# A transformer layer on one core: first loads by half rows with V's products among the maxima, and last chunks in a new order with spread steps and buffers of their own

## The chip, the core and the metric

The kernel runs on one core of a Trainium2 chip. The core has a matrix engine (TensorE, PE in the profile, with PEld for its weight loads), a vector engine (VectorE, DVE), a scalar engine (ScalarE, ACT), GpSimd (POOL) and SyncE (SP), which here only issues DMAs. Each engine takes its instructions strictly in the order of the program; between engines semaphores say what must wait. DMAs are issued on SP's queue or on ACT's and are carried out by 16 DMA engines. The metric is the time of one execution in microseconds (us).

## The reference

One layer with 8 sequences of 1024 positions and width 256, everything in float32: attention with 16 heads of 16, with a fixed bell-shaped prior added to the scores, a residual and a layer norm without weights; then a feed-forward part with ternary weights, a low-rank branch and a squared ReLU, again with residual and norm. Cut to what matters:

```
Q, K, V = heads(x @ Wq.T + bq), heads(x @ Wk.T + bk), heads(x @ Wv.T + bv)
scores  = Q @ K.T / sqrt(16) + prior_lambda * gaussian_mask(L)
out     = softmax(scores) @ V                       # 16 heads
x       = layernorm(x + out @ Wo.T + bo)
h       = bitlinear(x, w_fc) + gate * (x @ v.T @ fast_b.T @ u.T)
r       = maximum(h, 0)
x       = layernorm(x + bitlinear(r * r, w_proj))
# bitlinear(x, w): s = mean|w| per row; x @ (clip(round(w / s), -1, 1) * s).T
```

## The kernel before

**Operands in parts.** Operands of many products are held as two float32r tiles: `hi`, the rounded value, and `lo`, what the rounding left. Queries and keys of four heads (a "group" G; 32 of them, four to a sequence) stand in the "stack": tiles `stack[name, s, pr, a]` (`st_q`, `st_k` in the profile) of 128 partitions by 1024 positions, two slots `s = G % 2`, each tile with one head's parts in 64 rows and two rows beside them for the row maxima. The parts go through DRAM: the projection gives a tile `two` (hi and lo), `write_parts` (L187 to L197) writes it to `parts_q` or `parts_k` in the order the stack needs (two DMAs for keys, three for queries), and `fill_stack` (L287) reads it back, 8 DMAs of 256 KB to a group.

**The start (L92 to L337).** x of sequence 0 is loaded in two halves (L99), the four weights on ACT's queue (L106), the biases behind the first x half on SP's queue. TensorE turns weights and x by transposes (`turn_weights`, `first_turn`), and `first_part` (L199) makes the key and query parts of the first eight heads, half by half of the positions: two ACT passes over the product (`full`, and `two`'s hi), then VectorE's subtraction for lo. The order of the calls is k and q of half 0, the second half of x, k and q of half 1. Only the parts of the first four heads are written at once; those of the next four (`second_heads`) are written after `fill_stack(0)`, whose key loads are on SP's queue and whose query loads are on ACT's. Then V for the whole of sequence 0 (L315 to L325: 32 matmuls, 8 additions of VectorE), `fill_stack(1)` and five small loads (L329 to L337). One of the `two` tiles of the start has the buffer named `junk`.

**The loop (L1463 on).** One pass `g` handles two blocks of 128 by 1024 exponentials (`exp_scores`, L698: matmuls L715, prior by matmuls L725 or by VectorE L738, exponential L739 on ACT) and the products with V of the pass before (`weigh`, L754). There are 512 passes. Twelve passes ahead (`LEAD`), `max_scores` (L634) makes the scores once more and `max_row` (L659) takes each row's maximum on VectorE, with an output tile nobody reads, also named `junk`; after every eight passes of this `set_max` (L671) transposes the maxima, negates them and sends them through DRAM into two rows of the query stack (one DMA out, L686, four back, L692). So the loop begins with 12 passes, g = -12 to -1, of maxima alone, the "lead-in".

**Pieces.** All other work (x transposes, projections, output projection, feed-forward) is cut into pieces `(cost, function, room, ready)` that stand in a list `jobs`. A pass takes pieces from the head while there is room (`halves`, the two halves of the PSUM bank `misc`) and the first one is ready. A piece issues its matmuls at once and returns `empty`, which issues the evacuation later in the pass. In the lead-in one piece is taken every second pass (two in the first): `load_x` of the next sequence and six of the eight key and query pieces of the second eight heads (`queries_keys`, L587). `defer(n, f)` puts a step off until n passes later. In the last 64 passes `own`, the list of pieces of the last sequence, follows when `jobs` is empty.

**The last sequence (`last_chunk`, L1109).** Its four chunks of 256 positions (e0 to e3) have pieces P (output projection, L1157, then VectorE's residual add L1160), T (transposes, L1185, to xhi and xlo), L (low-rank product, L1198, to `low`, L1211 on ACT and L1213 on VectorE), H (eight hidden pieces, L1236 with the low-rank term L1243; ReLU L1252 and square L1256 on ACT, product L1257 on GpSimd, lo L1258 on VectorE, once for two pieces) and O (two blocks of 128 positions in two parts each, L1272). After a block's second part VectorE multiplies and adds (L1281, L1282) and measures (L912, L913); after the second block GpSimd computes the inverse deviation of both (`norm_scale`, L917 and the power L918), and one unit later VectorE applies it to both (L1136) and one DMA writes 256 positions (L1290). Chunks 1 and 3 share buffers for xhi/xlo (`two`), `low` (the tile `prior`) and hi/lo (stack slot 0); chunks 0 and 2 share others.

**After the loop (L1545 on).** PSUM is one pool of eight banks, and the rest runs piece by piece in an order written out by hand: what is left of `own`, mixed with `divide_last(1)` (the last softmax sums, L874 to L899) and P of chunks 2 and 3; then H of chunk 1 with T and O of its neighbours, O of chunk 0, L of chunk 2 and so on, to H of chunk 3, O of chunk 2 and O of chunk 3. Every engine's instructions are tied to the order in which the program issues them.

## Time and profile before

| | us |
|---|---|
| median of three runs shown | 2251.11 (2249.8 to 2251.25) |
| profiled execution, its own time | 2246.88 |
| its span, first to last instruction | 2245.1 |
| first key and query loads of the stack issued | 23.75 |
| first matmul of the exponentials (L715, g = 0) | 69.58 |
| last products with V end | 2173.0 |
| last matmul ends | 2236.0 |

The granted TensorE clock is 0.99 on average over the span. How to read the lines shown: a line of the timeline has the start, the duration, the engine, the line of the kernel, the operation, the output and the inputs, the shapes, and the number of instructions that were merged (x4); in brackets stands how long the engine had been idle before it and what ended that. SPq and ACTq are the queues on which DMAs are issued, so that their lines show issues and not transfers. A line of a table of stretches has the stretch, its length, and for each engine its busy time in it and the number of instructions; then the granted clock (1.00 is full speed), the share of the DMA engines' time in use (just over 1 where packets overlap the edge of a stretch) and GB/s.

### The profile page before, as it was taken

Reading aid. Unit: us, or ns where it says so; the run is one execution under the profiler, and the core shown is the slowest. Engines: PE = TensorE matmul, PEld = TensorE weight load, DVE = VectorE, ACT = ScalarE, POOL = GpSimd, SP = SyncE. Lnnn points to the kernel's source line nnn. Section 1 sums busy time; section 2 is a strip of 40 time slices with the busy share of each in tenths; the row PEclk is TensorE's granted clock in tenths of the full one; section 3 lists DMA queues with packets and bytes.
Section 4 is the critical chain, followed back from the end, with each engine's and each line's share of the span. In section 5 each row is a group of like instructions: output and inputs, shape, how many; then the busy total and the mean of one; then the engine's idle time right before and its main releaser. Section 6 shows DMA issues by size and latency. Waiting matters only on the chain.

```text
span 2245.1 us, 36797 instructions
## 1 busy us (share of the span) xinstructions
PE 2167.9 (97%) x13144; PEld 1262.1 (56%) x13144; DVE 1591.8 (71%) x2959; ACT 1441.8 (64%) x2152; POOL 893.3 (40%) x1000
## 2 busy tenths in 40 slices
PE   6999999999999999999999999999999999999996
PEld 3444445565555655556555565555555555555556
DVE  5777777777777776777767777677777777677736
ACT  2466556766667667666666667676666666666654
POOL 3023232344324454344532444335443345345443
PEclk8899999999999999999999999999999999999998
DMA  8223233323343124423243223421344321422010
GB/s 204 91 76 109 59 73 124 90 72 71 100 116 105 37 74 116 131 68 78 69 131 104 73 67 89 131 85 52 74 119 122 78 73 52 139 56 58 23 35 20
DMA packets 110189, 193.36 MB, mean 86 GB/s; under 512 B 20973, under 2 KB 49981, under 8 KB 110005
## 3 DMA queue, kind: packets, MB, share of 16 engines
q1 hardware_dynamic: 108596, 188.91, 30.5%
q8 instruction: 104, 1.70, 0.3%
q10 hardware_dynamic: 1408, 2.10, 0.3%
q14 instruction: 81, 0.66, 0.1%
HBM read 105.19 MB, written 85.69 MB: 85 GB/s over the span
## 4 chain that ended last, share of the span: by engine, by line
PE 78%; DVE 8%; POOL 1%; ACT 1%; issue 1%; DMA 1%; SPq 0%; POOLq 0%; DVEq 0%; ACTq 0%
PE e L715 21%; PE av L754 18%; PE s L649 14%; DVE junk L661 5%; PE e L725 5%; PE misc L1028 4%; PE misc L1063 4%; PE misc L595 4%; PE misc L954 2%; PE misc L568 2%; PE misc L1035 1%; ACT exp L739 1%; DVE st L912 1%; PE misc L988 1%; PE misc L542 0%
## 5 line engine op out<-in xcount | busy, mean ns | idle before, releaser
L661 DVE CUSTOM_DVE_ANT_0 junk<-s,wide 128x1024 f32<-128x1024 f32 x1024 | 1248.7, 1219 | 534.7 <-PE s L649 483.7
L739 ACT ACTIVATE exp<-e 128x1024 f32<-128x1024 f32 x1024 | 1027.3, 1024 | 630.3 <-PE e L725 383.1
L715 PE MATMUL e<-st_q,st_k 66*128 66x512 f32 (+1 forms) x2048 | 666.1, 426 | 1.4 <-DVE pm L661 0.9
L715 PEld LDWEIGHTS e<-st_q,st_k 66*128 66x128 f32 (+1 forms) x2048 | 324.6, 189 | 464.4 <-ACT exp L739 81.8
L754 PE MATMUL av<-exp,v 128*17 128x512 f32 x4096 | 540.5, 599 | 0.0
L649 PE MATMUL s<-st_k,st_q 64*128 64x512 f32 x2048 | 403.6, 449 | 43.0 <-DVE pm L661 33.2
L649 PEld LDWEIGHTS s<-st_k,st_q 64*128 64x128 f32 x2048 | 168.1, 186 | 182.5 <-DVE pm L661 78.0
L738 DVE TENSOR_TENSOR e<-e,wide 128x372 f32<-128x372 f32 (+2 forms) x376 | 190.8, 508 | 53.9 <-PE e L715 48.6
L1046 POOL TENSOR_TENSOR rl<-rl 128x512 f32<-128x512 f32 x112 | 116.7, 1042 | 250.2 <-ACT hi L1045 243.7
L725 PEld LDWEIGHTS e<-prior,ident_r 128*128 128x128 f32 x1056 | 160.3, 190 | 24.3
L754 PEld LDWEIGHTS av<-exp,v 128*17 128x17 f32 x4096 | 68.0, 95 | 185.8 <-issue 183.1
L725 PE MATMUL e<-prior,ident_r 128*128 128x244 f32 (+2 forms) x1056 | 158.2, 272 | 0.0
L1048 POOL TENSOR_TENSOR lo<-rl,hi 128x512 fp32r<-128x512 f32 x112 | 145.4, 1298 | 8.8
L1083 POOL TENSOR_TENSOR r<-r,sp_row 128x256 f32<-128x256 f32 x56 | 41.1, 734 | 203.7 <-ACT r L1082 203.5
L578 POOL TENSOR_TENSOR v<-v,bv_row 128x256 f32<-128x256 f32 x56 | 38.5, 687 | 195.8 <-ACT v L577 195.8
L1028 PE MATMUL misc<-xhi,wfT 128*128 128x256 f32 x448 | 116.0, 282 | 0.2 <-ACT fullq L610 0.2
L1028 PE MATMUL misc<-xlo,wfT 128*128 128x256 f32 x448 | 115.1, 280 | 0.0
L1063 PE MATMUL misc<-wpT,lo 128*128 128x256 f32 x448 | 111.8, 283 | 2.1 <-POOL lo L1048 2.1
L1063 PE MATMUL misc<-wpT,hi 128*128 128x256 f32 x448 | 113.8, 287 | 0.0
L615 POOL TENSOR_TENSOR twok<-fullk,twok 128x512 fp32r<-128x512 f32 x30 | 39.0, 1300 | 187.1 <-ACT twok L614 187.1
L1041 ACT ACTIVATE rl<-misc,s_fc 128x256 f32<-128x256 f32 x224 | 94.1, 475 | 0.1
L1063 PEld LDWEIGHTS misc<-wpT,lo 128*128 128x128 f32 x448 | 85.0, 190 | 6.3 <-POOL lo L1048 2.9
(235 smaller groups left out, 2348.8 us busy)
## 6 DMA issues: line engine op xcount, KB each, us to landing
st_k<-parts_k SPq DMA_DIRECT2D x128, 256.0 KB
st_q<-parts_q SPq DMA_DIRECT2D x124, 256.0 KB
parts_k<-twok SPq DMA_DIRECT2D x60, 512.0 KB
parts_q<-twoq SPq DMA_DIRECT2D x64, 256.0 KB
parts_q<-twoq SPq DMA_DIRECT2D x30, 512.0 KB
x<-in_L_attn_x_dram SPq DMA_DIRECT2D x16, 512.0 KB
raw_o<-avs SPq DMA_DIRECT2D x248, 32.0 KB
rec<-back SPq DMA_DIRECT2D x30, 256.0 KB
```

Source lines behind the costliest of these rows:

```text
L649: nc.tensor.matmul(pair[a][:, kh, :], stack["q", s, pr, a][rows, ts(blk, P)], stack["k", s, pr, a][rows, ts(kh, HALF)], start=True, stop=True,
L661: nc.vector.tensor_tensor_reduce(out=junk, in0=t.rearrange("p k n -> p (k n)"), in1=wide[:, LEFT - P * blk : LEFT - P * blk + L], scale=1. ...
L715: nc.tensor.matmul(t[:, a, :], stack["k", s, pr, a][rows, ts(blk, P)], stack["q", s, pr, a][rows, ts(h, HALF)], start=True, stop=not by_pe,)
L725: nc.tensor.matmul(t[:, a, lo - HALF * h : hi - HALF * h], ident_r, prior[:, n, lo - first : hi - first], start=False, stop=(n == 1),)
L738: nc.vector.tensor_add(part, part, add.to_broadcast([P, 2, hi - lo]))
L739: nc.scalar.activation(e, t.rearrange("p a n -> p (a n)"), AF.Exp)
L754: nc.tensor.matmul(av[32 * j : 32 * j + HD + 1, :], v_bufs[b % 2][:, blk, g * HG + j, : HD + 1], es[j // 2][:, ts(j % 2, HALF)], start=(n ...
L1028: nc.tensor.matmul(ph, wfT[:, dc, ts(hc, P)], st[k2][:, dc, :], start=(dc == 0 and k2 == "xhi"), stop=False,)
L1041: nc.scalar.activation(rl[:, ts(k, n)], ph, AF.Relu, scale=s_fc[:, hc : hc + 1])
L1046: nc.gpsimd.tensor_mul(rl, rl, rl)
L1048: sub(lo, rl, hi.bitcast(F32))
L1063: nc.tensor.matmul(py, st[k][:, hc, ts(i, P)], wpT[:, hc, :], start=(hc == 0 and k == "hi"), stop=(hc == NHC - 1 and k == "lo"),)
```

## The change

**At the start.** Both halves of x are loaded first. Wq is scaled by 1/4 as it leaves PSUM, and the bias of q after it, so that no projection of q scales any more. `first_part` makes hi in one ACT pass and lo in one VectorE instruction from PSUM; the second half of x is turned between k and q of half 0, one of its four copies on VectorE. The four `two` tiles have the buffers `two`, one of the exponentials' (`e`), `o0` and `o1`. `fill_one` loads one stack tile or a range of its columns: for group 0 the keys whole on SP's queue and the first half of the queries on ACT's; then the last query part of half 1 is written, all parts of the next four heads, and the second half of the queries loaded.

**In the lead-in.** V of sequence 0 is made by the loop's own pieces (`values`: two matmuls in one bank half, an ACT copy, a GpSimd addition), taken in turn with the six key and query pieces and spread over the 12 passes; `load_x` of the next sequence stays in `jobs` for pass 0. The pieces stand behind the pass's scores and first maximum. `set_max` for the first eight passes comes one pass sooner, and half of its four loads go on ACT's queue. `fill_stack(1)` and the five small loads come at pass -2.

**At the end.** From seven passes before the last, `own` is mixed with what is left of `jobs`. Each block of 128 positions has its own inverse deviation, norm and output DMA; a block's residual add is measured at once; and an output's steps (multiply, add, measure, invert, finish) come 1, 2, 3, 5 and 6 units after its matmuls, for chunk 3 at once and one unit later. Chunk 3 gets `o0` and `rec` for xhi/xlo and `low`, chunk 2 stack slot 1 for hi/lo. The order after the loop is another: all T and L come ahead of the outputs, and the output parts of chunks 0 to 2 stand one by one between the hidden pieces of chunks 2 and 3.

```diff
     load_x(0, 0)
+    load_x(0, 1, "hi")
...
-    load_x(0, 1, "hi")
...
-    nc.vector.tensor_scalar_mul(bcol["q"], bcol["q"], qscale)
...
-        copy(t.rearrange("p c d -> p (c d)"), pt)
-        wT[name] = t
+        t = t.rearrange("p c d -> p (c d)")
+        if name == "q":
+            nc.vector.tensor_scalar_mul(t, pt, qscale)
+            nc.vector.tensor_scalar_mul(bcol["q"], bcol["q"], qscale)
+        else:
+            copy(t, pt)
...
-            nc.scalar.copy(xT[:, dc, ts(half, HALF)], pt)
+            copy = nc.vector.tensor_copy if dc == half == 1 else nc.scalar.copy
+            copy(xT[:, dc, ts(half, HALF)], pt)
...
-    def first_part(name, scale, half, tag, full):
+    def first_part(name, half, two):
...
+        nc.scalar.activation(two[:, 0, :], pt, AF.Identity, bias=bias)
+        nc.vector.scalar_tensor_tensor(
+            out=two[:, 1, :],
+            in0=pt,
+            scalar=bias,
+            in1=two[:, 0, :].bitcast(F32),
+            op0=ALU.add,
+            op1=ALU.subtract,
+        )
+        return two
...
-    turn_weights("q", nc.vector.tensor_copy)
-    first_part("k", 1.0, 0, "two", fulls[0])
-    first_part("q", qscale, 0, "junk", fulls[1])
+    turn_weights("q", None)
+    two = {}
+    def two_tile(name, half, pool, tag):
+        return pool.tile([P, 2, HALF], F32R, tag=tag, name=f"two{name}_0_0_{half}")
+    low, high = slice(0, P // 2), slice(P // 2, P)
+    two["k", 0] = first_part("k", 0, two_tile("k", 0, p1, "two"))
+    write_parts("k", parts_of["k", 0, 0], two["k", 0], 0, low)
     first_turn(1)
-    first_part("k", 1.0, 1, "o0", fulls[2])
-    first_part("q", qscale, 1, "o1", fulls[3])
+    two["q", 0] = first_part("q", 0, two_tile("q", 0, epool, "e"))
+    write_parts("q", parts_of["q", 0, 0], two["q", 0], 0, low)
+    two["k", 1] = first_part("k", 1, two_tile("k", 1, p1, "o0"))
+    write_parts("k", parts_of["k", 0, 0], two["k", 1], 1, low)
+    two["q", 1] = first_part("q", 1, two_tile("q", 1, p1, "o1"))
     turn_weights("v", nc.vector.tensor_copy)
     turn_weights("o", nc.scalar.copy)
     woT = wT["o"]
...
+    def fill_one(name, G, pr, a, queue, cols=slice(0, L)):
         (b, g), s = divmod(G, NG), G % SLOTS
-        assert made.get((b, g // 2)) == 2 * NHALF
+        at, src = P // 2 * a, HD * ((g % 2) * HG + 2 * pr + a)
+        queue.dma_start(
+            stack[name, s, pr, a][at : at + P // 2, cols].bitcast(F32),
+            parts_of[name, b, g // 2][src : src + HD, :, cols].rearrange("p l n -> (p l) n"),
+        )
...
+                for name in "kq":
+                    fill_one(name, G, pr, a, nc.sync)
+    halves_of_q = slice(0, HALF), slice(HALF, L)
+    for pr in range(NP):
+        for a in range(2):
+            fill_one("k", 0, pr, a, nc.sync)
+            fill_one("q", 0, pr, a, nc.scalar, halves_of_q[0])
+    write_parts("q", parts_of["q", 0, 0], two["q", 1], 1, low)
+    for (name, half), t in two.items():
+        write_parts(name, parts_of[name, 0, 0], t, half, high)
+    for pr in range(NP):
+        for a in range(2):
+            fill_one("q", 0, pr, a, nc.sync, halves_of_q[1])
+    def load_later():
+        nc.sync.dma_start(v_sb, v)
+        nc.sync.dma_start(fb_sb, fast_b)
+        nc.sync.dma_start(u_sb, u.rearrange("(c p) r -> p c r", p=P))
+        nc.sync.dma_start(gate_c, gate.partition_broadcast(P))
+        nc.sync.dma_start(bo_row, bo.partition_broadcast(P))
...
-                nc.sync.dma_start(row[at : at + 2, ts(h, HALF)], rows[:, j])
+                queue = nc.scalar if step == 0 and j % 2 else nc.sync
+                queue.dma_start(row[at : at + 2, ts(h, HALF)], rows[:, j])
...
+        def measure(mv, i, k):
+            norm_stats(st["r"], mv, i, f"{k}_{b}_{c}")
+        def invert(mv, i):
+            var = mv[:, i, 1:2]
+            nc.gpsimd.tensor_scalar_add(var, var, EPS)
+            nc.gpsimd.tensor_tensor(out=var, in0=var, in1=mhalf[:, :1], op=ALU.pow)
...
                 nc.vector.tensor_add(r[:, i, :], po, x1[:, i, :])
-                defer(1 + i, measure)
+                measure(mv, i, 1)
+                defer(1, lambda: invert(mv, i))
+                defer(2, apply)
+            def apply():
+                apply_norm(x1, mv, i)
                 if i == CT - 1:
-                    defer(2 + i, apply)
+                    st["normed"] = now
...
-                t = p1.tile([P, 2, NDC, n], F32R, tag="two", name=f"x12_{b}_{c}")
+                tag = "two" if c == 1 else "o0"
+                t = p1.tile([P, 2, NDC, n], F32R, tag=tag, name=f"x12_{b}_{c}")
...
-                if odd:
+                if c == 1:
                     t = prior.rearrange("p k n -> p (k n)")[:, :n]
                 else:
-                    t = p1.tile([P, n], F32R, tag="tern", name=f"low_{b}_{c}")
+                    tag = "rec" if odd else "tern"
+                    t = p1.tile([P, n], F32R, tag=tag, name=f"low_{b}_{c}")
...
-                    if odd:
-                        ab = [stack[name, 0, half, a] for a in range(2)]
+                    if c:
+                        ab = [stack[name, int(c == 2), half, a] for a in range(2)]
...
+                spaced = (1, 2, 3, 5, 6) if c < NCH - 1 else (0, 0, 0, 1, 1)
+                steps = multiply, add, lambda: measure(mv, i, 2), lambda: invert(mv, i), finish
+                for n, f in zip(spaced, steps):
+                    defer(n, f) if n else f()
+            def multiply():
                 nc.vector.tensor_mul(r[:, i, :], py, sp_row)
+            def add():
                 nc.vector.tensor_add(r[:, i, :], r[:, i, :], st["x1"][:, i, :])
+            def finish():
+                apply_norm(r, mv, i)
+                nc.sync.dma_start(out[b, ts(c * CT + i, P), :], r[:, i, :])
...
-                (0.23, lambda dc=dc: turn(dc), 1, lambda: st.get("normed", now) + 1 < now)
+                (0.23, lambda dc=dc: turn(dc), 1, lambda: "normed" in st)
...
+    v_first, qk_first, jobs[:7] = values(0, misc), jobs[1:7], jobs[:1]
+    early = [u for two in zip(v_first, qk_first) for u in two] + v_first[6:]
...
+        if g == -2:
+            fill_stack(1)
+            load_later()
...
-        if not jobs and g >= total - per_batch:
-            jobs, own = own, []
+        if g == total - 7:
+            old, jobs = jobs, []
+            while old and old[0][0] > 0.1 and old[0][2] == 0:
+                jobs.append(old.pop(0))
+            while old:
+                jobs += [own.pop(0), *old[:2]]
+                old = old[2:]
+            jobs, own = jobs + own, []
...
-        done = g + LEAD - 2
+        done = g + LEAD - (1 if g < 0 else 2)
...
         if g < 0:
-            if g % 2 == 0:
-                work += [jobs.pop(0)[1] for _ in range(2 if g == -LEAD else 1)]
+            n = g + LEAD + 1 - (done >= QSTEP - 1)
+            upto = 14 * n // (LEAD - 1)
+            if halves == 2:
+                work += [early.pop(0)[1] for _ in range(len(early) - 14 + upto)]
...
-        empties = [piece() for piece in work]
+        empties = [piece() for piece in work] if g >= 0 else []
         if g + LEAD < total:
             pair, blk, pm = max_scores(g + LEAD)
             max_row(pair[0], blk, pm[:, 0:1], f"{g + LEAD}_0")
+            if g < 0:
+                empties = [piece() for piece in work]
             rest = pair[1], blk, pm[:, 1:2], f"{g + LEAD}_1"
...
-    h1, h2, h3 = (k["H"] for k in (e1, e2, e3))
-    jobs = [*jobs[:1], last[0], *jobs[1:4], last[1], *jobs[4:6], *e2["P"], *jobs[6:8], *e3["P"], *jobs[8:]]
-    jobs += [*h1[:2], *e2["T"], *h1[2:4], *e0["O"], *e2["L"], *h1[4:], *e3["T"], *h2[:4]]
-    jobs += [*e1["O"], *e3["L"], *h2[4:], *h3, *e2["O"], *e3["O"]]
-    for u in jobs + [gap]:
+    h1, h2, h3, o0, o1, o2, o3 = (k[n] for n, k in zip("HHHOOOO", (e1, e2, e3, e0, e1, e2, e3)))
+    jobs = [*jobs[:1], last[0], *jobs[1:4], last[1], *jobs[4:7], *e2["P"], *jobs[7:8], *e3["P"], *jobs[8:]]
+    jobs += [*h1[:2], *e2["T"], *h1[2:4], *e2["L"], *e3["T"], *h1[4:6], *h2[:2], *e3["L"], *h1[6:]]
+    side = [*o0, *o1, *o2]
+    for k, u in enumerate(h2[2:] + h3):
+        jobs += [u, *(side[k : k + 1])]
+    jobs += [*side[k + 1 :], *o3]
+    for u in jobs + 7 * [gap]:
```

## The prediction

> **What bounds the kernel now.** I read the table of engines first, then stretches of the first 80 us and of the last 75 us, then single instructions in them. TensorE is busy 97% of the span, so the long middle is bound by matmuls and the change leaves it alone; only the two ends, where TensorE idles or runs at half clock, can give anything.
>
> ```profile
> PE 2167.9 (97%) x13144; PEld 1262.1 (56%) x13144; DVE 1591.8 (71%) x2959; ACT 1441.8 (64%) x2152; POOL 893.3 (40%) x1000
> ...
> 23.75 2.51 SPq L296 DMA_DIRECT2D st_k<-parts_k  x4
> 26.41 2.85 ACTq L296 DMA_DIRECT2D st_q<-parts_q  x4
> 32.55 0.47 PE L649 MATMUL s<-st_k,st_q 64*128 64x512 f32 x1 [1.90 <-DMA st_q<-parts_q]
> 38.34 1.23 DVE L661 CUSTOM_DVE_ANT_0 junk<-s,wide 128x1024 f32<-128x1024 f32 x1 [8.20 <-DMA parts_q<-twoq]
> ```
>
> See two waits in series. The first scores wait until 32.55 for the loaded queries. Then the first maximum waits until 38.34, although its scores lie ready: its output tile `junk` shares its buffer with the query part that was being written to DRAM, and that write stood in the queue behind the loads.
>
> ```profile
> core 0: us, PE busy (x) PEld busy (x) DVE busy (x) ACT busy (x) POOL busy (x), PEclk, DMA share, GB/s
> 28.00:38.30 10.30, 2.90 (x12) 1.35 (x10) 1.24 (x3) 0.47 (x1) 0.00 (x0) 0.80 0.96 266
> 38.30:69.50 31.20, 22.93 (x64) 11.01 (x64) 27.12 (x44) 4.64 (x10) 4.28 (x4) 0.72 0.74 195
> 69.50:75.20 5.70, 5.62 (x16) 3.85 (x16) 3.02 (x5) 2.52 (x3) 0.00 (x0) 0.50 0.35 133
> ...
> 2173.00:2180.00 7.00, 4.64 (x27) 4.01 (x28) 3.38 (x11) 2.17 (x5) 0.93 (x2) 0.84 0.00 0
> 2180.00:2204.50 24.50, 23.07 (x155) 19.68 (x153) 16.07 (x35) 12.56 (x28) 8.09 (x10) 0.98 0.01 1
> 2204.50:2208.50 4.00, 0.20 (x2) 0.00 (x0) 2.77 (x5) 1.18 (x4) 2.98 (x4) 1.00 0.00 0
> 2208.50:2219.30 10.80, 10.77 (x76) 10.57 (x76) 6.19 (x15) 5.50 (x12) 3.09 (x5) 0.84 0.08 26
> 2219.30:2222.00 2.70, 0.00 (x1) 0.00 (x0) 2.64 (x4) 0.89 (x2) 1.98 (x2) 1.00 0.00 0
> 2222.00:2236.00 14.00, 13.66 (x100) 13.46 (x100) 6.85 (x14) 5.92 (x12) 5.04 (x6) 0.88 0.06 20
> 2236.00:2245.10 9.10, 0.00 (x0) 0.00 (x0) 4.18 (x12) 0.00 (x0) 1.23 (x3) 0.68 0.16 58
> ```
>
> The columns are stretch, its length, busy time of each engine (instructions), granted clock, DMA. From 38.3 to 69.5 VectorE sets the pace: 24 maxima, 1.37 us from one to the next, 27.1 of 31.2 us busy. The first group of exponentials runs at clock 0.50. At the end there are two holes in TensorE (3.8 and 2.7 us), each followed by matmuls at a lowered clock, and 9.1 us after the last matmul. What makes a hole:
>
> ```profile
> 2205.79 1.04 POOL L1257 TENSOR_TENSOR rl<-rl 128x512 f32<-128x512 f32 x1
> 2205.86 2.16 DVE L1136 TENSOR_SCALAR xT<-xT,mv,rstd 128x256 f32<-128x256 f32 x2 [1.14 <-POOL rstd L918]
> 2208.53 0.58 PE L1243 MATMUL ph<-low,lowT 128*128 128x256 f32 x1 [3.84 <-DVE low L1213]
> ```
>
> VectorE waits in order 1.14 us for GpSimd's power, then needs 2.16 us for two normalizations beside GpSimd's products (the same two took 0.73 us at 2236.34 with GpSimd idle), and `low`, which TensorE needs, stands behind.
>
> **The lead-in, step by step.** The key part of half 0 takes one ACT pass instead of two: 11.54 + 0.69 (ACT) + 0.69 (DVE) gives its writes at 13.0 instead of 13.56. The second half of x is transposed before the queries (1.04 us of PE), so the query part is there at about 15.9 instead of 15.24; its three issues take 2.85 us (0.57 + 1.05 + 1.23), to 18.9, and the key part of half 1, ready at 17.9, is issued to 20.1. SP no longer issues the last query part (20.80 to 23.64) before the loads. A write landed 2.8 us after its issue (23.64 to ACT's 26.41), so the key loads start at 22.9 instead of 23.75, and the query halves on ACT's queue at 21.7 instead of 26.41. The first scores need two key tiles and two query halves. Before, 2 MB landed between 23.75 and 33.5, 215 GB/s. Until the second key tile there are 0.5 MB of keys and 0.5 MB of query halves, a quarter MB of them ahead of 22.9: 3.7 us, and some 1.7 us to land, gives 28.3; the maximum begins at about 29.0. The query part now lies in a buffer of the exponentials, so nothing holds `junk`: the 8.2 us wait goes. First maximum 38.34 to 29.0: **-9.3**. Bounds: 27 (no landing time) and 33 (the 6.1 us from issue to 32.55 taken from 22.9, and 4 us of DMA disorder): -11 to -5.
>
> Then twelve steps of two maxima. V's eight pieces now lie here: each 4 matmuls (1.02 to 1.13 us at full clock, 2.08 at half, the rows of L595, same shape), an ACT copy (0.47, row L610) and a GpSimd add (0.687, row L578) in place of VectorE's 0.42. VectorE's eight adds stood in the empty stretch 23 to 29, so dropping them saves nothing by itself. A step needs about 1.0 us of scores and 14/11 x 1.1 us of pieces, 2.4 us of PE at full clock against VectorE's 2.75: hidden, with PE 87% full; at half clock 4.4 to 4.8. As the pieces now stand behind the scores in PE's order, the small waits of the maxima (31.2 - 22 x 1.373 = 1.0 us) can go. Against that PE is empty from about 20 to 27.5, V having left that gap, and starts at half clock: in the trace, after PE stood from 34.2 to 38.3, the clock is 0.50 from 36 to 44 and full again from 46. Two steps at half clock cost 2 x (3.7 - 2.75) = 1.9. Net **+0.5**, bounds -1 to +6.
>
> [...]
>
> The row maxima's way back to the stack (set_max, PE 61.25, rows issued 63.38, second hop from 65.87, first exponential matmul 69.58: 8.3 us) now starts a step sooner by its number but still only when the eighth pair is done; two of its four hops go to ACT's queue, where V's copies wait behind them. `fill_stack(1)` (8 loads, 5 us of issue) and the five small loads move from before the lead-in to two steps before its end; behind them in SP's queue stand the next key part and the next batch's x. Group 4 needs the stack at about 78, it lands near 69; x lands near 75 and is wanted near 75, as `load_x` now comes first in group 0 and shifts the pieces by one group. Taken **+0.5**, bounds 0 to +4. With PE warm, the group at half clock (5.7 us from 69.5) takes about 4.5: **-1.2**, bounds -2 to 0. Lead-in: -9.3 + 0.5 + 0.5 - 1.2 = **-9.5**.
>
> **The end.** The work on PE after the last weighing (2173.0) at full-clock rows: 32 hidden pieces x 0.583, 16 output parts x 0.96, 4 projections x 1.69, transposes 1.8, low-rank 1.9, the last division 1.3: 46 us. It took 63.0, to 2236.0: 10.7 idle (stretches above), the rest, 6.3, lowered clock. The new order makes every low-rank product before the outputs, in tiles of their own, and an output's steps are spread over six units, so VectorE no longer waits for the power with `low` behind it. The two holes (6.5) go, and of the 2.4 idle us before 2180 I take 1.5, because chunk 0's transposes and low-rank now fit into groups 510 and 511: -8.0. Of 6.3 of lowered clock 2 stay: -4.3. Added: the last output part now waits for its own squares, with no other output between: ACT 0.47 + 0.63, GpSimd 1.04, VectorE 0.69 and hand-overs 0.3, less the 0.96 part in front: +2.2. VectorE becomes full: 36.5 us of its rows, plus up to 0.7 for each normalization beside GpSimd, in some 50 us, and GpSimd gets 8 more powers (0.94 each): +2.5, bounds 0 to +8. The drain: add, statistics and norm of one block instead of two, 128 KB last instead of 256: 9.1 to 6.7, -2.4. Loop lengthened by 0.6, products moved into it 0.9: -0.3. Tail: -8.0 - 4.3 + 2.2 + 2.5 - 2.4 - 0.3 = **-10.3**, bounds -16 to -3.
>
> **Sum.** -19.8: span 2245.1 to about 2225, the profiled execution 2246.88 to 2227. The median shown, 2251.11, lies 4.2 above that execution; I shift it alike: 2231.
>
> **Rivals.** (1) The loads stay the limit: DMA is 96% busy from 28 to 38, and the first scores come at 33 whatever the order. Against it: only half as many bytes are needed first, and the `junk` wait of 5.3 us behind the scores goes anyway. Lead-in -5, all 2236. (2) The end is bound by VectorE and the order of GpSimd's powers and products: single normalizations wait as the pairs did. For it: 16 waits where there were 8; against it: the spread leaves a power three units or more. Tail -3, all 2238. (3) Slower: the lead-in is bound by PE at half clock. Place: the twelve steps; price: a step takes 2.4/clock, 4.8 at 0.50, 11.5 x 2.05 = +23.6 against the term of +0.5, so 2254. It decides once the clock of the stretch is below 0.53. For it: 0.50 for most of the 10 us from 51; against it: the mean there is 0.72 with PE at 73%, and fuller stretches (75 to 80) run at 1.00. (4) The pieces don't come earlier, since `ready` refuses them in the last seven groups: about -2 less, inside the forecast's range.
>
> **How the numbers follow.** Forecast 0.66 (2223 to 2237), rival 1 0.10, rival 2 0.14, rival 3 0.06, and 0.04 for more gain than I see. The range for 8 in 10, with the bounds of start (-5) and end (-3) not both taken: 2220 to 2241. What a measurement tells from no change is 0.2%, 4.5 us: faster 0.91, within 0.03, slower 0.06.
>
> **What would show it.** First maximum near 29 with no DMA before it (step 1); maxima 1.37 us apart, clock over 0.8 from the third step (step 2); first exponential matmul near 60 (step 3); no hole over 1 us on PE between the last weighing and the last hidden piece, then one of about 2 us (end); about 6.7 us from the last matmul to the end. I am wrong if PE waits for x or the stack in groups 0 to 4, or if VectorE is over 90% busy in the end.

## The result, and the profile after

The changed kernel takes 2232.31 us (median of 4 runs, 2227.59 to 2233.07), the kernel before 2250.79 (4 runs, 2249.8 to 2251.25): a ratio of 0.991, 95% interval 0.9896 to 0.9924. The profiled execution took 2231.73, its span 2229.9, which is 15.2 us under the profile before; the prediction's sum was 19.8.

The engine line of the page after:

```profile
PE 2160.5 (97%) x13144; PEld 1258.9 (56%) x13144; DVE 1591.5 (71%) x2952; ACT 1442.7 (65%) x2155; POOL 902.7 (40%) x1024
```

And single instructions of its first 30 us (start, length, engine, line, tiles, the wait in front):

```profile
18.89 2.78 ACTq L298 DMA_DIRECT2D st_q<-parts_q  x4
21.60 2.42 SPq L298 DMA_DIRECT2D st_k<-parts_k  x4
...
25.78 0.76 PE L647 MATMUL s<-st_k,st_q 64*128 64x512 f32 x1 [8.73 <-DMA st_k<-parts_k]
...
27.74 1.22 DVE L659 CUSTOM_DVE_ANT_0 junk<-s,wide 128x1024 f32<-128x1024 f32 x1 [6.30 <-PE s L647]
```

Scores and maximum no longer wait in series for two transfers: the scores begin 6.8 us sooner (32.55 to 25.78), and the first maximum follows them at once, 10.6 us sooner (38.34 to 27.74).

The same stretches as before, of the profile after (length, busy time of each engine, granted clock, DMA share and GB/s):

```profile
20.00:27.70 7.70, 1.56 (x4) 0.78 (x4) 1.29 (x4) 0.00 (x0) 0.00 (x0) 0.60 0.95 235
27.70:59.60 31.90, 28.27 (x102) 16.16 (x101) 27.90 (x45) 7.17 (x17) 8.32 (x10) 0.88 0.70 197
59.60:65.30 5.70, 5.19 (x22) 3.04 (x21) 4.71 (x9) 4.14 (x6) 1.33 (x2) 1.00 1.08 201
2164.30:2171.60 7.30, 5.32 (x44) 5.02 (x42) 2.65 (x7) 4.14 (x10) 1.97 (x2) 1.00 0.00 0
2171.60:2184.00 12.40, 12.08 (x69) 8.98 (x67) 8.20 (x21) 5.20 (x12) 6.25 (x12) 1.00 0.01 1
2184.00:2186.20 2.20, 0.13 (x1) 0.00 (x0) 2.20 (x4) 0.84 (x2) 0.71 (x1) 0.86 0.00 0
2186.20:2192.40 6.20, 6.15 (x29) 6.15 (x30) 2.20 (x5) 3.73 (x8) 1.95 (x2) 0.50 0.00 0
2192.40:2214.90 22.50, 22.50 (x189) 22.28 (x188) 15.50 (x30) 13.29 (x27) 12.45 (x17) 1.00 0.06 20
2214.90:2219.90 5.00, 0.74 (x4) 0.53 (x4) 4.50 (x10) 0.27 (x1) 2.54 (x4) 0.98 0.09 33
2219.90:2223.60 3.70, 3.69 (x19) 3.69 (x19) 2.02 (x7) 0.00 (x0) 1.56 (x4) 0.56 0.08 27
2223.60:2229.90 6.30, 0.26 (x3) 0.05 (x1) 2.42 (x7) 0.00 (x0) 0.77 (x2) 0.73 0.18 62
```

The lead-in's maxima still take VectorE 27.9 us; TensorE beside them is fuller (28.3 of 31.9 us) at clock 0.88, and the first group of exponentials runs at 1.00 instead of 0.50. In the end the old holes of 3.84 and 2.70 us are gone, and there are new ones: 2.1 us at 2184, then half clock for 6.2 us, and 4.3 us in the five from 2214.9. While VectorE has 4.50 of 5.00 us of work there, TensorE stands.

Where the 15.2 us lie follows from the start of each group's first exponential, after against before: 10.7 us sooner at group 0, 12.7 at group 2, 13.2 at group 68, 9.3 at group 76, 10.0 at group 504, 9.0 at group 511. The span ends 15.2 sooner. So the lead-in gave 12.7, the place at groups 68 to 76 took 3.9 back, 1.2 were won elsewhere on the way, and from group 504 on 5.2. This is the place that took back:

```profile
348.19 0.47 PE L647 MATMUL s<-st_k,st_q 64*128 64x512 f32 x1 [0.94 <-PE misc L540]
348.60 0.62 ACT L612 CAST twoq<-fullq 128x512 fp32r<-128x512 f32 x1 [2.66 <-DMA parts_k<-twok]
349.12 1.93 ACT L738 ACTIVATE exp<-e 128x1024 f32<-128x1024 f32 x2
...
350.19 1.22 PE L647 MATMUL s<-st_k,st_q 64*128 64x512 f32 x3 [1.53 <-ACT exp L738]
```

ScalarE's rounding of the query parts (L612) waits until the key parts, which lie in the same buffer `two`, are written to DRAM. The exponentials stand behind it on ScalarE, the next scores wait for a bank that an exponential must free, and TensorE is empty for 1.53 us; then its clock is 0.51 for 6 us. The 0.94 us in front aren't due to this wait: they are as long where the rounding doesn't wait (`own_part` below, at 351.48). Before, the same wait is there, 1.44 us long (L614 at 360.62), TensorE is empty for 0.94 + 0.31 us, and the clock stays 1.00.

### The profile page after: what moved, and what is told of

It reads as the page before. It is cut to its first block, busy times and chain, and to the rows that moved or that the text cites. A ratio compares the mean times of both kernels' runs of the same rounds, so it can differ in the third digit from the quotient of the medians.

```text
span 2229.9 us, 36851 instructions
## 1 busy us (share of the span) xinstructions
PE 2160.5 (97%) x13144; PEld 1258.9 (56%) x13144; DVE 1591.5 (71%) x2952; ACT 1442.7 (65%) x2155; POOL 902.7 (40%) x1024
## 4 chain that ended last, share of the span: by engine, by line
PE 82%; DVE 8%; POOL 1%; issue 1%; ACT 1%; DMA 1%; SPq 0%; POOLq 0%; DVEq 0%; ACTq 0%
PE e L714 22%; PE av L753 19%; PE s L647 15%; DVE junk L659 6%; PE e L724 5%; PE misc L1027 4%; PE misc L593 4%; PE misc L1062 4%; PE misc L953 2%; PE misc L566 2%; PE misc L1034 1%; ACT exp L738 1%; DVE st L911 1%; PE misc L987 1%; PE misc L540 0%
## 5 line engine op out<-in xcount | busy, mean ns | idle before, releaser
L576 POOL TENSOR_TENSOR v<-v,bv_row 128x256 f32<-128x256 f32 x64 | 43.8, 686 | 213.4 <-ACT v L575 213.4
```

## The experiments

All times are set against runs of the kernel before on the same chip. "Tail" is the time from the start of the last weighing's matmuls (the last that read `exp` and `v`) to the span's end: 72.7 us before, 66.2 after.

**The changed kernel again, and each part alone.** No edit in the first; the second and third take the lead-in's or the end's lines of the diff.

> The changed kernel once more. In its first profile TensorE stood 2.47 us at 347 to 350 us (ScalarE's rounding L612 waits 2.66 us for the write of the key parts, exponentials behind it) and then ran at clock 0.50 to about 356: the lead over the kernel before falls there from 13.2 to 9.4 us. Theory C (chance: the DMA round trip in front of it fell late): in some executions the stall is as short as before, the times are of two kinds some 4 us apart, 2227.5 and 2232, and the profile may show either. Theory D (the change itself makes the stall): it is in every execution, all times 2231 to 2233.

Measured: 2229.72 (2226.86 to 2231.87), ratio 0.9912 (0.9891 to 0.9933). The four times are 2226.86, 2228.06, 2231.38 and 2231.87. The profile (2228.06) shows both places of interest once more, the first by instructions and the stretch behind them, the second by stretches:

```profile
347.47 0.62 ACT L612 CAST twoq<-fullq 128x512 fp32r<-128x512 f32 x1 [1.50 <-DMA parts_k<-twok]
...
349.07 0.73 PE L647 MATMUL s<-st_k,st_q 64*128 64x512 f32 x3 [0.37 <-DMA rec<-back]
...
350.00:353.40 3.40, 3.40 (x13) 1.70 (x6) 2.07 (x4) 1.58 (x3) 0.68 (x1) 0.50 0.87 309
```

```profile
2182.40:2184.60 2.20, 0.08 (x1) 0.00 (x0) 2.20 (x4) 0.86 (x3) 0.67 (x1) 1.00 0.00 0
2184.60:2190.80 6.20, 6.03 (x48) 5.79 (x49) 2.85 (x6) 5.64 (x14) 3.09 (x3) 1.00 0.00 0
```

The wait at L612 is 1.50 here, TensorE is empty for 0.94 + 0.37 us, the clock is halved for 3.4 us behind it where it was for 6.8, and 1.7 us are lost in place of 3.9. The hole in the end is as long as it was (2.13 us), and the clock behind it is 1.00 where it was 0.50: the tail is 64.2 instead of 66.2. Theory C fits: two profiles of the same program pay different prices at both places, and the four times fall into two pairs, though four times are few.

> The kernel before with the lead-in's part of the change alone (its end as before). By the traces the lead-in is worth 12.7 to 13.2 us up to group 68. Theory C: the median falls by that, 2238. Theory D: it gives 3.5 back in groups 68 to 76, 2241. By the prediction's own sum (-9.5): 2241 as well, but with the first maximum near 29 and the lead at group 20 at 9.5 and not 12.7. First exponential matmul near 59.7 in any case.

Measured: 2238.31 (2237.04 to 2239.29), 0.9951 (0.9932 to 0.997), 11 us under the kernel before. Its first maximum came at 29.98, and the lead was 9.1 us at group 2 and 11.1 at group 60, with nothing lost at groups 68 to 76 (11.4 behind them). The start varies: the first key part comes off TensorE at 10.19 us in the first profile of the changed kernel, at 10.71 in the second and at 11.86 here, and the first maximum follows it (27.74, 27.90, 29.98); what makes it vary is not shown.

> The kernel before with the end's part of the change alone. By the traces the end is worth 5.2 us (lead 10.0 at group 504, 15.2 at the end), of 10.3 predicted. If the two parts add up: 2245.5. Rival (the prediction's sum holds for the end and something of the lead-in's part took it away): 2240.5. In its profile the stretch after the last weighing has the steps of VectorE 3.5 us apart as in the changed kernel.

Measured: 2243.69 (10 runs, 2239.7 to 2246.33), 0.9971 (0.9961 to 0.9981), 5.7 us under the kernel before. Tail 63.9, the same holes as with the whole change (2.13, 2.19 and 2.08 us), and 1.1 us lost between group 504 and the last weighing. The profiled execution was the fastest of the ten. The parts add up: 11 + 5.7 is 16.7, the whole was 18.5 in the first comparison and 19.6 in the second, each to some 3 to 5 us by its interval.

**The lead-in: one buffer, the half rows, V.**

> The kernel before with one buffer moved: the query part of half 0 lies in a buffer of the exponentials instead of the maxima's. Nothing else. Theory: the first maximum waits only for its scores (33.04 instead of 38.34, matmuls 33.04 + 0.97), so it begins near 33.7 and all that follows comes 4.6 us sooner: 2246. Rival (the loads behind it or VectorE's next wait take the place): first maximum sooner, first exponential matmul still near 69.6, time within 1 us of 2250.8.

```
-    first_part("q", qscale, 0, "junk", fulls[1])
+    first_part("q", qscale, 0, "e", fulls[1], epool)
```

Measured: 2248.28 (10 runs), 0.9993 (0.9982 to 1.0004): no difference, as the rival has it. The first maximum came at 34.98, 3.4 us sooner, and the first exponential matmul at 68.06, 1.5 sooner. What took the place, in order of time on ScalarE and TensorE of this kernel:

```profile
59.98 0.62 ACT L614 CAST twoq<-fullq 128x512 fp32r<-128x512 f32 x1 [8.77 <-DMA parts_k<-twok]
60.50 0.47 ACT L610 ACTIVATE fullk<-misc,bk 128x256 f32<-128x256 f32 x1
...
61.02 0.38 PE L677 MATMUL misc<-ident,pm 128*16 128x128 f32 x1 [3.48 <-ACT fullk L610]
```

The rounding that waits at group 70 waits here too, 8.77 us, for writes issued at 53.7 and 54.8 that land at about 60, with DMA 0.88 to 0.95 busy up to 61. A key piece behind it holds the `misc` bank, and the transpose of the maxima waits for that bank. So the buffer alone gives nothing that shows: the transpose's results leave ScalarE at 61.44, where they left it at 61.67 before. The wait shown at L661 was the first of two that end at the same place.

> The changed kernel with the queries' rows loaded whole for the first group, behind the write of the second half, as before the change (all else of the lead-in as changed). The prediction's step: the half rows let the loads start at 18.9 instead of behind the write of half 1 (issued to 20.5, landed near 23.3), and a score came 6.1 us behind its loads' issue: first scores 29.5 instead of 25.8, first maximum 30.5 to 31 instead of 27.8, time +2.5 to +3 on 2229.7, 2232.5. Rival (the stretch is bound by DMA, 95% busy, and what comes first doesn't matter for the end of the lead-in): first exponential matmul within 1 us of the changed kernel's 59.7.

```
+    write_parts("q", parts_of["q", 0, 0], two["q", 1], 1, low)
     for pr in range(NP):
         for a in range(2):
             fill_one("k", 0, pr, a, nc.sync)
-            fill_one("q", 0, pr, a, nc.scalar, halves_of_q[0])
-    write_parts("q", parts_of["q", 0, 0], two["q", 1], 1, low)
+            fill_one("q", 0, pr, a, nc.scalar)
...
-            fill_one("q", 0, pr, a, nc.sync, halves_of_q[1])
```

Measured: 2235.14 (2231.7 to 2240.93), 0.993 (0.9908 to 0.9953). Query loads and first scores of this kernel:

```profile
25.05 2.85 ACTq L298 DMA_DIRECT2D st_q<-parts_q  x4
...
30.86 0.76 PE L643 MATMUL s<-st_k,st_q 64*128 64x512 f32 x1 [13.04 <-DMA st_q<-parts_q]
...
33.24 1.22 DVE L655 CUSTOM_DVE_ANT_0 junk<-s,wide 128x1024 f32<-128x1024 f32 x1 [11.33 <-PE s L643]
```

The first maximum is 5.3 us later than in the second profile of the changed kernel, and the first exponential matmul 4.0 (65.10 against 61.09). In the nine profiles with half rows and V beside the maxima these two lie from 27.74 to 29.98 and from 59.66 to 63.25, so the order of the bytes is worth 3.3 to 5.5 us of the one and 1.9 to 5.4 of the other. By the ratios it is some 4 us of the time, and their intervals overlap. It is more than expected at least in part because the three issues of the second query write take 3.8 us of SyncE (18.57 to 22.38) where those of the first took 2.1 (15.05 to 17.11), and the loads stand behind them.

> The changed kernel with V of the first sequence back in the gap in front of the lead-in (eight pieces on TensorE, VectorE adding the bias), the six query and key pieces left beside the maxima. The prediction's step: V beside the maxima is hidden and costs 0.5 at most for a cold clock, so V in the gap changes the time by -1 to +0.5: clock 1.00 at 20 to 28, no wait of 0.94 in front of the third maximum. Rival G (V in the gap delays the first scores, which stand behind it on TensorE, and the maxima, behind eight adds on VectorE): first maximum 1 to 3 us later, time by as much.

```
+    for tp in range(NB // 2):
...
-    early = [u for two in zip(v_first, qk_first) for u in two] + v_first[6:]
+    early = qk_first
```

Measured: 2231.03 (2229.1 to 2233.3), 0.9913 (0.9895 to 0.9931). First maximum 28.37, no wait before the third (maxima 1.38 apart), clock 1.00 at 20 to 28; 24 maxima take 32.56 us from first to last, against 32.46 and 32.65 in the two profiles of the changed kernel, and 32.66 before. Neither a cost nor a gain of V beside the maxima shows.

**The middle: the shared buffer.**

> The changed kernel with a buffer of their own for the query parts of the first two sequences (instead of the one that the key parts are written from), so that ScalarE's rounding L612 doesn't wait for the key parts' write, with the exponentials behind it. Between groups 60 and 100 the kernels with the changed lead-in lost up to 4.5 us against the profile before (3.8, 1.7, 4.6, 3.9, 2.4, 2.1 us, and 0.4 with the lead-in alone), always at that wait. Theory C (that wait alone, its length by chance): the loss between groups 60 and 100 is under 0.5 us and the time is some 2.5 us under the changed kernel's 2229.7 to 2232.3, 2228. Rival H (the wait only moves on to the next user of the buffers or of SyncE's queue): loss and time as they were.

```
-                two = p1.tile([P, 2, HALF], F32R, tag="two", ...)
+                two = p1.tile([P, 2, HALF], F32R, tag="lo" if name == "q" and b < 2 else "two", ...)
```

Measured: 2230.47 (2229.11 to 2236.61), 0.9928 (0.991 to 0.9946). In the profile L612 runs at 349.26 with no wait in front, and from group 68 to 76 the lead grows by 0.7 us. The profiled execution is the slowest of the four nevertheless: holes of 1.2 to 2.1 us elsewhere were followed by a low clock in it, such as this one at group 26, 1.96 us long in every profile with the changed lead-in; the first line is this kernel's, the second the changed kernel's in its second profile:

```profile
166.90:172.90 6.00, 6.00 (x29) 2.96 (x33) 3.12 (x6) 3.48 (x6) 0.00 (x0) 0.72 0.27 106
```

```profile
166.60:172.60 6.00, 5.96 (x38) 2.98 (x39) 4.64 (x10) 3.47 (x6) 0.00 (x0) 1.00 0.29 111
```

So the wait goes and the loss with it, as theory C says, but the median of four runs doesn't show it, and the wait alone isn't the price. Over the nine other profiles with the shared buffer and the changed lead-in, groups 68 to 76 cost from 4.6 us to nothing (the kernel with the lead-in alone gained 0.4 there, which the expectation counts as a loss). In `side_later` L612 waits 1.49 us and the loss is 0.1; in the changed kernel's second profile it waits 1.50 and the loss is 1.7. The difference is the clock: 1.00 behind the wait in the one, halved for 3.4 us in the other.

**The end: whose order sets the pace.** How one output's steps lie beside the products, in the changed kernel's first profile, and the two last holes:

```profile
2207.32 1.04 POOL L1261 TENSOR_TENSOR rl<-rl 128x512 f32<-128x512 f32 x1
2207.39 1.12 DVE L1142 TENSOR_SCALAR xT<-xT,mv 128x256 f32<-128x256 f32 x1 [0.41 <-POOL mv L1139]
...
2217.09 0.39 PE L1276 MATMUL py<-wpT,st_k 128*128 128x256 f32 x1 [2.19 <-DVE st_k L1262]
...
2219.91 0.58 PE L1276 MATMUL py<-wpT,st_k 128*128 128x256 f32 x1 [2.08 <-DVE st_k L1262]
```

A normalization waits 0.41 us for the power, then takes 1.12 beside a product (0.38 to 0.41 alone), and the rests L1262 that TensorE needs stand behind it. The steps come 3.47 us apart. The normalization starts 0.07 us behind the product and ends 0.15 us behind its end; why the pair is slow, no run here shows.

> The changed kernel with the second normalization of chunks 0 to 2 as one ScalarE pass (scale 1/s, bias -mean/s, the bias by one VectorE instruction on 128x1) instead of one VectorE pass of 1.12 us beside GpSimd's products. Theory E (in the end VectorE's order sets the pace: its steps come 3.47 us apart, TensorE's two hidden pieces and one output take 3.09): the steps fall to about 3.1 us apart, the two last holes of TensorE (2.19 and 2.08 us, both waits for the rounding rests L1262 behind a normalization) lose some 1 us each: 3 to 4 us less than the changed kernel's 2229.7 of the same chip, about 2226.5. Rival F (TensorE sets the pace until 48.9 us behind the last weighing, VectorE's rhythm only looks like it; the last holes are the chain relu, square, product, rest): not more than 1 us.

```
             def finish():
-                apply_norm(r, mv, i)
+                if c < NCH - 1:
+                    nc.vector.scalar_tensor_tensor(out=mv[:, i, 0:1], ...)
+                    nc.scalar.activation(r[:, i, :], r[:, i, :], AF.Identity, bias=..., scale=...)
```

Measured: 2237.2 (2235.18 to 2237.9), 0.9935 (0.992 to 0.9951): 5 to 7.5 us slower than the changed kernel, against an expected gain of 3. Tail 68.2. ScalarE, in order, now waits where VectorE did, and five times as long:

```profile
2209.57 0.60 ACT L1303 ACTIVATE xT<-xT,mv 128x256 f32<-128x256 f32 x1 [2.12 <-DVE mv L1299]
```

Its relus and squares stand behind that wait, and the steps came 4.1 us apart (2209.57, 2213.70, 2217.80). The expectation had counted busy time on ScalarE and not asked what its order would hold up; so it tests neither E nor F as it was meant to.

> The changed kernel with the second normalization one step later (steps 1, 2, 3, 5, 7 instead of 1, 2, 3, 5, 6), so that VectorE doesn't wait 0.42 us for GpSimd's power in front of it. Theory E: six times 0.4 us less, 2227.5; the wait in front of L1142 is gone in the profile. Rival F: within 0.7 us of 2229.7.

```
-                spaced = (1, 2, 3, 5, 6) if c < NCH - 1 else (0, 0, 0, 1, 1)
+                spaced = (1, 2, 3, 5, 7) if c < NCH - 1 else (0, 0, 0, 1, 1)
```

Measured: 2228.87 (2227.06 to 2230.92), 0.99 (0.9885 to 0.9916). The tail fell from 64.2 in the changed kernel's second profile to 61.7 us, with the same hole of 2.12 and the same clock in front, and the wait before L1142 is gone:

```profile
2209.30 0.43 DVE L1295 TENSOR_TENSOR xT<-xT,wide 128x256 f32<-128x256 f32 x1
2209.69 1.12 DVE L1142 TENSOR_SCALAR xT<-xT,mv 128x256 f32<-128x256 f32 x1
```

VectorE is busy 11.73 of 12 us in this stretch (10.38 in the changed kernel), and its steps are 3.0 us apart. But TensorE is never empty here, nor in the changed kernel (12.00 of 12 us in both), and its last hidden piece has its last matmul 47.5 us behind the start of the last weighing in both, and in `act_norm` too. So rival F is right up to there: TensorE sets the pace, two hidden pieces and an output part in 3.09 us. VectorE, at 3.47, falls behind it, and that comes due in the last holes: the last of the rests L1262 begins at 53.18 us in the changed kernel, at 51.05 here and at 57.34 in `act_norm`, counted alike. In this form theory E holds. The two last holes (2.19 and 1.99 us) become one of 1.72; of the 2.4 us of tail some 0.7 are time at half clock that is less. The median is not separated from the changed kernel's.

> The kernel with the late normalization (steps 1, 2, 3, 5, 7), and chunk 2's transposes moved ahead of four hidden pieces instead of two, so that VectorE has two pieces more to make the transposed rest before the low-rank product needs it. Theory E (the hole of 2.12 us, 20 us behind the last weighing, is that rest standing behind a normalization of 1.13 us and two rests of squares on VectorE): the hole shrinks to under 1 us, the time from the last weighing to the end falls from 61.75 to about 60, and no half clock after it: 2227. Rival (the chain, not VectorE's order, makes it late, or the hole comes back at the next low-rank product): 61.75 stays.

```
-    jobs += [*h1[:2], *e2["T"], *h1[2:4], *e2["L"], *e3["T"], *h1[4:6], *h2[:2], *e3["L"], *h1[6:]]
+    jobs += [*e2["T"], *h1[:4], *e2["L"], *e3["T"], *h1[4:], *h2[:2], *e3["L"]]
```

Measured: 2225.93 (2224.86 to 2228.07), 0.9905 (0.9889 to 0.9922). Tail 58.8, and the hole shrank to 1.25 us, not under 1. Of the 3.0 us less of tail 1.8 are idle time of TensorE; 1.7 are the half clock behind the last hole of `late_norm` (0.50 from 2217.8 to 2221.1), which doesn't come behind the same hole here (1.67 us, clock 1.00) and so may be luck; the drain is 1.0 longer. By the ratios of the times it isn't faster than `late_norm` (0.9905 and 0.99). The row of the hole:

```profile
2185.80 0.39 PE L1201 MATMUL plow<-xlo,v_st 128*128 128x256 f32 x1 [1.25 <-DVE xlo L1192]
```

> As the one before, and the output parts of chunks 0 to 2 go beside the hidden pieces two pieces later, so that the last one lies behind the last hidden piece and not before the last two. Theory E: the last hole (1.72 us with the late normalization, waiting for the rests of the last squares) is filled with an output part of 0.96 us, and from the last weighing to the end it is about 59; but the steps of the last output of chunk 2 (to the 7th unit) now lie in the end's gaps, which may give 0.5 us back: 2226 to 2227. Rival: VectorE is full (3.9 of 4 us) and every delay of its work comes out at the end: 61 to 62.

```
-        jobs += [u, *(side[k : k + 1])]
-    jobs += [*side[k + 1 :], *o3]
+        jobs += [u, *(side[k - 2 : k - 1] if k > 1 else [])]
+    jobs += [*side[k - 1 :], *o3]
```

Measured: 2227.06 (2225.35 to 2227.45), 0.9906 (0.9891 to 0.9921). Tail 57.9, the last hole 0.6 us instead of 1.7; from the last matmul to the end it takes 7.6 us instead of 7.2. The times of this kernel and the one before it overlap, so the 0.9 us is the trace's alone.

> The late normalization, the early transposes and the query parts' own buffer together. Theory C with E: the seam's loss between groups 68 and 76 (3 to 4.6 us in five profiles of kernels with the shared buffer, a gain of 0.7 with the own one) goes, the end stays at 58.8 us from the last weighing: 1 to 3 us under turns_early's 2225.9, so 2223 to 2225, if no half clock falls elsewhere. Rival (what the seam loses is lost by chance, to a clock that falls behind any hole of over 1 us, and a hole less doesn't show in the median): 2225 to 2227.

The kernel that ran holds the edit of side_later as well, so it is late_norm, turns_early, side_later and own_part in one. Measured: 2223.87 (2223.3 to 2225.74), 0.9885 (0.9868 to 0.9903). Tail 58.0, and the lead grows by 0.7 us from group 60 to group 100 where the changed kernel lost 3.8. It is the fastest of all that ran. Its interval overlaps that of the first comparison by 0.0007; what the own buffer adds to the rest isn't separated from the spread of the executions.

## Why the prediction was right, point by point

The time was 2232.31 for 2231 predicted, inside the narrow range. That it is so near is luck, as errors cancel: lead-in 3.2 us better in the profile, the middle 2.7 worse (the 3.9 lost and the 1.2 won above), the end 5.1 worse, and the step from profile to median off by 3.6 the other way, since the profiled execution before lay 3.9 under its median (2246.88 and 2250.79) and the one after only 0.6 (2231.73 and 2232.31).

**First maximum, -9.3.** Right in mechanism and size: 10.6 in the first profile, and 8.4 to 10.6 in nine profiles with the half rows and V beside the maxima. The query halves were issued at 18.89 (21.7 in the working), the key loads at 21.60 (22.9). Undoing the half rows cost 3.3 to 5.5 us of it; the buffer alone gives 3.4, and nothing that shows in the time. The 1.7 us to land in the working are a guess that no run shows by itself; the first scores came 4.2 us behind the issue of the key loads (25.78 and 21.60), for 5.4 in the working.

**Steps +0.5.** Right: 24 maxima take 32.46 us (32.66 before), with one wait of 0.94 at clock 0.50. The stretch counted in the working, 38.3 to 69.5, holds 22 of the 24 maxima. V's place shows no difference. **Way back +0.5 and half-clock group -1.2.** The lead at the first exponential matmul was 9.9 (69.58 to 59.66), so of the 10.6 at the first maximum and the 0.2 of the steps the way back cost 0.9; at group 2 it was 12.7, so the groups at full clock gave 2.8 and not 1.2, the term that was mis-sized. No wait for x or the stack appeared in groups 0 to 4.

**The middle unchanged.** This failed: the wait at L612 was in the profile before, and I didn't ask what a transfer later by 1 us would make of it, nor what a clock that falls behind it costs (3.4 to 6.8 us at half clock where it fell).

**The end, -10.3.** The sign held, the size did not: 5.2 in the first profile, 7.4 in the second, 7.7 with the end's part alone (5.7 by its median). By terms, from the stretches above: idle time of TensorE from the last weighing to the last matmul went from 10.7 to 8.7 us (-2.0), where the prediction had -8.0 for holes, +2.2 for the last squares and +2.5 for a full VectorE, together -3.3. Of its signs, "no hole over 1 us" failed: 1.30 and 2.12 us stand between the last weighing and the last hidden piece. The step that failed in it is "the spread leaves a power three units or more", which was said against rival 2. The power is given one unit, and one normalization of 1.12 us in front of a rest makes VectorE late: late_norm took 2.4 us of tail back, turns_early 3.0 more, the changes in half clock included.

Lowered clock was mis-sized most, -4.3 predicted. Its 6.3 us were what the sum left over and not read from the clock; by the clock TensorE lost 4.9 us in the tail before, 4.7 in the first profile after (6.2 us at 0.50 and 3.7 at 0.56) and 2.4 in the second. So it gave 0.2 and 2.5. Behind the last matmul it was 9.1 us and is 6.3, -2.8 for -2.4. The pieces moved into the last groups cost 1.3 there (the lead falls from 10.0 at group 504 to 6.3 at group 508, and 8.7 of it are left at the last weighing) and take 1.3 of full-clock work out of the tail, so nothing for -0.3.

**Rivals.** (1) The loads as the limit: no, the first scores came at 25.78; but junk_only shows that for the first maximum they were the second wait in line. (2) VectorE and GpSimd's order: its mechanism is in the last holes, as `late_norm` and `act_norm` show, and its price was too high; up to them TensorE sets the pace. (3) TensorE at half clock in the lead-in: no, clock 0.88. (4) The pieces do come earlier.

## What to carry to other kernels

Take a wait away only after looking for the next one that ends at nearly the same time: a buffer that held up a maximum gave nothing alone, as the next wait, of a rounding for a write, ended where the work had stood before. In an engine that works in order, a step that waits for another engine belongs a unit later than the price of its input suggests; one place of delay took 2.4 us off the trace's tail, while handing the step to a less busy engine lost 5 because that engine waited in order as well. And when a sum is made from one profile, ask behind which of its short holes the clock could fall: at two such places the two profiles of the changed kernel differ by 2.0 us of tail (66.2 against 64.2) and by 2.2 us of loss (3.9 against 1.7).

## What the runs showed of the hardware

The clock behind a short hole isn't a property of the program. The hole of 2.1 us in the end is the same in eight profiles; the mean clock of the 6 us behind it was 0.50, 0.72 and 0.72 in three, and 1.00 in five (0.50 and 1.00 in the two of the changed kernel). Behind the hole of 1.96 us at group 26 it was 0.72 to 0.74 in six of eleven. Behind one of 1.17 us near 1930 us it was 0.57 to 0.72 in three of eleven. A low clock behind the hole in the end cost 2.0 us of tail (66.2 against 64.2), so a few such places could make the spread of the changed kernel's times (2226.9 to 2233.1).

What goes with it can be read from the clock records of the traces. In each run the clock changes only at multiples of 3.41 us: in the first profile at 2185.58, 2192.41, 2219.72, 2223.13 and 2226.54, which are 2, 8, 1 and 1 such slots apart. So 0.72 over 6 us is one slot at half clock and 0.50 two. Over the 14 profiles, a slot at full clock in which TensorE was busy for under 45% was followed by half clock in 53 of 53 cases, one with 45% to 70% in 34 of 106, and one with more in 1 of 8805; in `before` and `after` alone that is 9 of 9, 6 of 15 and none of 1257. Back to full clock it went behind 65 of 73 slots with TensorE busy for 95% or more (10 of 11 in these two), and behind none of 43 with under 80% (none of 8). So in these profiles a fall goes with how a hole lies in the slots. Of the hole of 1.96 us at group 26, 1.59 us or more lay in one slot in the six profiles where the clock fell, and at most 1.10 in the five where it stayed. For the hole of 2.1 us the two kinds overlap a little (1.45 to 2.13 us in one slot where it fell, 1.21 to 1.64 where it stayed). Where the slots begin differs from run to run (the first at 0.05 us of the span before and at 1.05 of the first one after), and no experiment here moves a hole within them on purpose.

In these profiles the clock also fell where TensorE had not stood for a whole slot: behind holes of 1.2 to 2.1 us, and behind all 32 slots with TensorE busy for 20% to 45% (6 of 6 in `before` and `after`).
